# A convolution stage in which one more of eight shifted copies of its input is made on chip instead of being loaded, with the order of the copies changed

## The chip, the cores and the metric

The kernel runs on one core of one Trainium2 chip. The time is device time in microseconds of one execution; the time shown for a kernel is the median of its runs. Besides these runs there is one execution that was taken with the hardware profiler, and everything said of engines, waits and transfers comes from it.

## The reference: a filter over the whole image, then a 3x3 layer

The input x holds 4 images of 512 x 512 positions with 16 channels, fp32. Two layers follow each other, each added to what it got:

```python
# layer 0: zero-padded to twice the size
X = jnp.fft.rfft2(x, s=(2 * l1, 2 * l2), axes=(-3, -2))          # x = _gn(x), 8 groups of 2 channels
Y = jnp.einsum('...hwi,ijhw->...hwj', X, H_full)                 # H_full = h0 + spectrum of the filter
y = jnp.fft.irfft2(Y, s=(2 * l1, 2 * l2), axes=(-3, -2))[..., :l1, :l2, :]
...
# layer 1: 3x3 cosine convolution of _gn(x)
y = conv(x, kernel / kernel_norm) / input_norm
y = 1.0 - jnp.arccos(y) * (2.0 / jnp.pi)
y = y * (jnp.tanh(kernel_norm / radius) * jnp.tanh(input_norm / radius)) + bias
```

_gn is a group normalization. The filter's spectrum is that of a filter between every input and output channel, a quotient of two polynomials in both directions. So the first layer is a two-dimensional linear convolution of 512 x 512 images by 512 x 512 filters, 16 x 16 of them. It is the first layer's product over channels that takes most of the time.

## The kernel before

The work is in stages, one after the other: the filter's spectrum along one axis (filter_phase), the input's transform along that axis (forward_phase), the stage that the change touches (conv_phase, line 650), and the last stage (last_phase) with the way back and layer 1. Tiles have 128 partitions (P). A scheduler orders the instructions of each engine from the program's text, the data's dependencies and the buffers of the pools; each engine then runs its own list in order, and waits for others by semaphores.

conv_phase works on 513 rows, one for each frequency along the first axis (the first frequency has two). For each row it convolves along the other axis: 64 pieces of the filter and 64 of the input, cut up as 8 by 8 to suit the tiles. The steps of a row n, each with its place:

- load_x (L697) and load_g (L685) fetch the row's input and filter from DRAM, on SP's queue.
- turn_x (L708) makes the row's rotated transform matrix: an ACT operation (turn, L718) and a DVE operation (L720).
- x_part (L723) transforms the input: 4 matmuls (L731) into px, two tiles of PSUM, each evicted into place 0 of the tile xe. evict (L678) gives every third eviction to DVE (L681), the others to ACT (L683).
- xe (L727) is 128 partitions by 8 places by 1,024 values. The 128 partitions of place 0 are 8 blocks of 16 channels. Taken together with xl, the same values multiplied by a fixed phase, they form a list of 256 rows, and place e must hold rows 16e to 16e + 127 of that list. So each place is the list seen 16 rows further on.
- x_late (L738) makes xl on POOL: four multiplications (L752), one over the whole tile (L753), one addition (L754). It also stores place 0 and xl to a DRAM scratch of 256 rows, xf_d, by two DMAs (L745) on POOL's queue. The pool of xl has one buffer, that of xe three, xf_d is fourfold.
- half_shift (L760) fills place 4: its lower 64 partitions from the upper half of place 0, its upper 64 from the lower half of xl. Both are copies on ACT (L763) of 64 x 1,024 values.
- load_xe (L766) fills places 1 to 3 and 5 to 7 from xf_d with two DMAs on SP's queue of 1,536 KB each; the second stands behind load_g's on the queue.
- g_part (L775) transforms the filter: 32 matmuls (L783, in four groups of 8 of two halves each) into tiles pg, three banks of PSUM, evicted into gh.
- mix (L792) is the product: 32 x 4 matmuls (L799) of gh with all eight places of xe, into pm, two banks, evicted to yf in four portions.
- over_q (L812) and over_g (L842) transform back: 16 transposes (L820) into pz; then an ACT copy zq (L827) and five DVE operations (L828 to L832) for every fourth; two POOL operations zd and z (L836, L838); 8 matmuls of two halves (L857) into py, evicted to yo, and a DMA to y_d on POOL's queue (L868). px, pz and py share three banks of PSUM.

step (L876) puts these together for five rows at once, in four quarters (k = 0 to 3): mix of row n, g_part of n + 1, over_q of n - 1, x_part and x_late of n + 2 at k = 0, half_shift of n + 2 at k = 2 and 3, turn_x of n + 3, over_g of n - 2. The scheduler may depart from this where an engine is free; in the built program ACT's order in a row (from one row's px to the next) is: xe eviction, lower half of place 4, yf, turn, gh, zq, upper half of place 4, yf, gh, zq, yo, yf, gh, zq, yf, gh, zq. POOL's is: two L752, store of place 0, two L752, L753, L754, store of xl, store of y, zd, z.

Of the kernel before, what the change touches and what calls it, by code (L numbers as in the profile page):

```python
# [46 lines left out]
P = 128  # L47
N = 512
B = 4
C = 16  # L50
# [6 lines left out]
XF = F * 2 * B  # L57
# [128 lines left out]
def load_const(nc, pool, cst, name, shape=None):  # L186
    src = cst[name]
    t = pool.tile(list(src.shape), F32, name=f"c_{name}")
    nc.sync.dma_start(out=t, in_=src)
    return t  # L190
# [10 lines left out]
def bc(ap, axis, shape):  # L201
    return ap.unsqueeze(axis).to_broadcast(shape)
# [447 lines left out]
def conv_phase(tc, cst, g_d, x_d, y_d):  # L650
    nc = tc.nc
    with ExitStack() as ctx:
# [15 lines left out]
        late = load_const(nc, cp, cst, "late").rearrange("p (v f) -> p v f", v=3)  # L668
# [4 lines left out]
        rows = [(0, 0, 0), (0, 0, 1)] + [(n // P, n % P, None) for n in range(1, N)]  # L673
        n_rows = len(rows)
        state = {}
# [9 lines left out]
        def load_g(n):  # L685
            rc, r, plane = rows[n]
            g = io.tile([P, C, 8 * C], F32, name="g")
            t, w = g.rearrange("p j x -> p (j x)"), C * 8 * C
            if plane is None:
                nc.sync.dma_start(out=t, in_=dram(g_d[rc], r, 0, [w, P], [1, w]))  # L690
            else:
                for to, at in ((0, (0, 96)[plane]), (64, (64, 32)[plane])):
                    nc.sync.dma_start(out=t[to : to + 32], in_=dram(g_d[rc], r, at * w, [w, 32], [1, w]))
                    nc.gpsimd.memset(t[to + 32 : to + 64], 0.0)
            state["g", n] = g

        def load_x(n):  # L697
            rc, r, plane = rows[n]
            x = io.tile([P, B, 8 * C], F32, name="x")
            t, w = x.rearrange("p b x -> p (b x)"), B * 8 * C  # L700
            if plane is None:
                nc.sync.dma_start(out=t, in_=dram(x_d[rc], r, 0, [w, P], [1, w]))
            else:
                nc.gpsimd.memset(t[S:], 0.0)
                nc.sync.dma_start(out=t[:S], in_=dram(x_d[rc], r, plane * S * w, [w, S], [1, w]))
            state["x", n] = x
# [16 lines left out]
        def x_part(n, b):  # L723

            if b == 0:

                state["xe", n] = xep.tile([P, 8, F, 2, 2, 2], F32, name="xe")  # L727
            if b % 2 == 0:
                state["px"] = ps_f.tile([P, 2, F, 2], F32, name="px", tag="full")
            px = state["px"]  # L730
            nc.tensor.matmul(px[:, b % 2].rearrange("p f c -> p (f c)"), state["x", n][:, b],  # L731
                             state["dfs", n], start=True, stop=True)
            if b % 2:
                evict(state["xe", n][:, 0, :, b // 2], px.rearrange("p k f c -> p f c k"))
            if b == B - 1:
                del state["x", n], state["dfs", n]

        def x_late(n):  # L738

            xe = state["xe", n][:, 0]  # L740
            fl = xe.rearrange("p f h c k -> p f (h c k)")

            def store(half, t):
                at = slice(C, P) if half == 0 else slice(0, P - C)
                nc.gpsimd.dma_start(out=xf_d[n % 4][half * P :, :][at], in_=t[at].rearrange("p f x -> p (f x)"))  # L745

            store(0, fl)
            xl = xlp.tile([P, F, 2, 2, 2], F32, name="xl")
            u = xlp.tile([P, F, 2, 2, 2], F32, name="xu")
            for c in range(2):  # L750
                for h in range(2):
                    nc.gpsimd.tensor_mul(u[:, :, h, c], xe[:, :, h, 1 - c], bc(late[:, 1 + c], 2, [P, F, 2]))  # L752
            nc.gpsimd.tensor_mul(xl.rearrange("p f h c k -> p f (h c k)"), fl, bc(late[:, 0], 2, [P, F, 8]))  # L753
            nc.gpsimd.tensor_add(xl.rearrange("p f h c k -> p (f h c k)"),  # L754
                                 xl.rearrange("p f h c k -> p (f h c k)"),
                                 u.rearrange("p f h c k -> p (f h c k)"))
            store(1, xl.rearrange("p f h c k -> p f (h c k)"))
            state["xl"] = xl

        def half_shift(n, half):  # L760

            dst, src = ((slice(0, 64), state["xe", n][64:, 0]), (slice(64, P), state["xl"][:64]))[half]
            nc.scalar.copy(state["xe", n][dst, 4].rearrange("p f h c k -> p (f h c k)"),  # L763
                           src.rearrange("p f h c k -> p (f h c k)"))

        def load_xe(n):  # L766
            src = xf_d[n % 4]
            for t in (1, 5):
                nc.sync.dma_start(
                    out=state["xe", n][:, t : t + 3].rearrange("p t f h c k -> p t (f h c k)"),  # L770
                    in_=bass.AP(tensor=src.tensor, offset=src.offset + t * C * XF,
                                ap=[[XF, P], [C * XF, 3], [1, XF]]),
                )

        def g_part(n, j):  # L775


            if j % 4 == 0:
                state["pg"] = [ps_g.tile([P, 4, F], F32, name=f"pg{c}", tag="pg") for c in range(2)]
            g, pg = state["g", n], state["pg"]  # L780
            for c in range(2):
                half = slice(64 * c, 64 * c + 64)
                nc.tensor.matmul(pg[c][:, j % 4], g[half, j], dg[half], start=True, stop=True)  # L783
            if j == 3:
                state["gh", n] = ghp.tile([P, F, 2, C], F32, name="gh")
            if j % 4 == 3:
                for c in range(2):
                    evict(state["gh", n][:, :, c, j - 3 : j + 1], pg[c].rearrange("p j f -> p f j"))
            if j == C - 1:
                del state["g", n]  # L790

        def mix(n, g):  # L792

            if g % 8 == 0:
                state["pm"] = ps_m.tile([P, 8, 8, 2 * B], F32, name="pm")
            xe, gh, pm = state["xe", n], state["gh", n], state["pm"]
            for q in range(4):
                f = g + 32 * q
                nc.tensor.matmul(  # L799
                    pm[32 * q : 32 * q + 32, g % 8], gh[:, f].rearrange("p c j -> p (c j)"),  # L800
                    xe[:, :, f].rearrange("p t h c k -> p t (h c k)"), start=True, stop=True,
                )
            if g == 7:

                state["y", n] = yp.tile([P, 16, 32, 4], F32, name="yf")
            if g % 8 == 7:
                evict(state["y", n][:, :, g - 7 : g + 1].rearrange("p t g x -> p g t x"),
                      pm.rearrange("p g t (h x) -> p g (t h) x", h=2))
            if g == 31:
                del state["xe", n], state["gh", n]  # L810
# [65 lines left out]
        def step(n):  # L876


            def row(k):
                return 0 <= n + k < n_rows  # L880

            if row(3):
                load_x(n + 3)
            if row(2):
                load_g(n + 2)
            if row(1):
                load_xe(n + 1)
            for k in range(4):
                if row(0):
                    for g in range(8):  # L890
                        mix(n, 8 * k + g)
                if row(1):
                    for j in range(4):
                        g_part(n + 1, 4 * k + j)
                if row(-1):
                    for t in range(4):
                        over_q(n - 1, 4 * k + t)
                if row(2) and k == 0:
                    for m in range(B):
                        x_part(n + 2, m)  # L900
                    x_late(n + 2)
                if row(2) and k >= 2:
                    half_shift(n + 2, k - 2)
                if row(3) and k == 2:
                    turn_x(n + 3)
                if row(-2) and k == 2:
                    for m in range(4):
                        over_g(n - 2, m)

        for n in range(-3, n_rows + 2):  # L910
            step(n)
# [443 lines left out]
```

## Time and profile before

| what | value |
|---|---|
| median of 3 runs | 19,007.57 us (19,006.79 to 19,023.34) |
| profiled execution: time, span | 19,054.31 us, 19,052.5 us |
| mean granted TensorE clock | 0.957 |
| PE, DVE, ACT, POOL busy, share of the span | 91%, 60%, 51%, 61% |
| 7,400 to 12,000 us (in conv_phase): PE, DVE, ACT, POOL busy | 4,116, 2,503, 2,423, 2,927 us of 4,600 |
| same stretch: busy share of the DMA engines, GB/s | 0.87, 321 |
| loads of xe: count, size, median from issue to landing | 1,026, 1,536 KB, 10.3 us |
| conv_phase: first and last L731 matmul | 6,953 us, 16,004 us |

The profile counts an engine as busy while it computes; issuing DMAs does not count. A group's line gives the source line, the engine, the operation, the output and the inputs by tile names, the shapes, and the count; then busy us and the mean ns of one; then how long the engine was idle just before, and what ended that. In a timeline each row has the start in us, its length in us and the instruction; a bracket holds the idle time before it. "issue" is idle time that ended with no wait that the profile shows. PEld is the loading of weights, which overlaps PE's matmuls.

### The profile page before, as it was taken

What the parts mean: (1) busy time and instruction counts of PE and PEld (TensorE: products, weight loads), DVE (VectorE), ACT (ScalarE), POOL (GpSimd) and SP (SyncE); (2) the same over time, 40 slices, a digit from 0 to 9 for tenths busy, and PEclk for the clock granted to TensorE, in tenths of its full rate; (3) what the DMA queues carried; (4) which work ended last, traced back from release to release, by engine and by line L of the source; (5) the groups of instructions that cost most, each with busy time, mean ns of one, the idle gap of its engine ahead of it and who ended that gap; (6) DMA issues with size and microseconds to landing.
All of it is one profiled execution on the core that took longest, in us unless ns stands there. A gap on an engine that the chain in (4) does not pass through costs nothing. (4 is left out here: it accounts for less than half of the span.)

```text
span 19052.5 us, 536690 instructions
## 1 busy us (share of the span) xinstructions
PE 17293.1 (91%) x227020; PEld 12605.2 (66%) x227020; DVE 11398.8 (60%) x23961; ACT 9747.4 (51%) x17871; POOL 11564.3 (61%) x12445
## 2 busy tenths in 40 slices
PE   8899999999999988898888888888888888979999
PEld 5455555555554457777777777777777776868888
DVE  8877777777763335555555555555555554347656
ACT  4455555555552235555555555555555553107777
POOL 7577777777771126666666666666666664127655
PEclk7899999999999999999999999999999999999999
DMA  3755455555557668888888888888888887796321
GB/s 100 206 153 148 137 150 150 146 139 149 149 151 223 187 211 320 323 322 324 320 322 317 322 327 317 322 324 323 320 325 323 321 320 282 268 321 210 131 72 62
DMA packets 2918658, 4543.39 MB, mean 238 GB/s; under 512 B 117442, under 2 KB 2086300, under 8 KB 2809374
## 3 DMA queue, kind: packets, MB, share of 16 engines
q1 hardware_dynamic: 2686062, 3768.91, 58.5%
q0 software_dynamic: 174896, 605.89, 8.3%
q10 hardware_dynamic: 55296, 134.24, 2.1%
q8 instruction: 1789, 29.31, 0.6%
q14 instruction: 615, 5.04, 0.1%
HBM read 3031.23 MB, written 1477.31 MB: 237 GB/s over the span
## 5 line engine op out<-in xcount | busy, mean ns | idle before, releaser
L783 PE MATMUL pg<-c_dg,g 64*128 64x128 f32 x32832 | 2842.9, 291 | 320.9 <-ACT gh L683 159.5
L799 PE MATMUL pm<-xe,gh 128*32 128x64 f32 x131328 | 2403.4, 222 | 576.2 <-issue 353.1
L799 PEld LDWEIGHTS pm<-xe,gh 128*32 128x32 f32 x131328 | 2012.8, 110 | 1180.2 <-issue 996.4
L783 PEld LDWEIGHTS pg<-c_dg,g 64*128 64x128 f32 x32832 | 2283.2, 190 | 662.7 <-issue 262.5
L372 PE MATMUL pg<-c_dinv,sp 128*128 128x256 f32 x8192 | 2278.4, 426 | 294.3 <-ACT st L377 193.8
L828 DVE TENSOR_TENSOR z<-zq,pz 128x256 f32<-128x256 f32 x2052 | 862.0, 420 | 2617.2 <-ACT zq L827 2534.6
L348 DVE RECIPROCAL dn<-dn 128x256 f32<-128x256 f32 x1024 | 1790.8, 1749 | 778.3 <-POOL dn L341 778.0
L372 PEld LDWEIGHTS pg<-c_dinv,sp 128*128 128x128 f32 x8192 | 1609.9, 207 | 946.8 <-ACT st L377 215.3
L681 DVE COPY gh<-pg 128x512 f32<-128x512 f32 x2046 | 1410.5, 689 | 1294.1 <-PE pg L783 1289.6
L417 PE MATMUL pt<-ev_in,c_todd 128*128 128x512 f32 x4096 | 1970.1, 606 | 45.6 <-DMA ev_in<-g_d 27.0
L752 POOL TENSOR_TENSOR xu<-xe,c_late 128x256 f32<-128x256 f32 x2052 | 1393.4, 705 | 856.3 <-ACT xe L683 832.3
L335 ACT COPY ab<-pab 128x512 f32<-128x512 f32 x2048 | 1104.2, 592 | 1130.1 <-POOL m L355 333.3
L683 ACT COPY yf<-pm 128x512 f32<-128x512 f32 x2046 | 1210.5, 592 | 919.0 <-PE pm L799 904.3
L377 ACT COPY st<-pg 128x256 f32<-128x256 f32 x2048 | 1072.6, 623 | 1024.0 <-PE pg L372 619.3
L763 ACT COPY xe<-xl 64x1024 f32<-64x1024 f32 x513 | 538.8, 1050 | 1877.0 <-POOL xl L754 1877.0
L350 POOL TENSOR_TENSOR x<-ab,ab 128x256 f32<-128x256 f32 x1024 | 875.8, 855 | 933.6 <-ACT ab L335 907.0
L1208 PE MATMUL pc<-l_band,xn 128*128 128x160 f32 (+3 forms) x9024 | 1374.8, 309 | 65.0 <-DVE e_o L1255 64.0
L683 ACT COPY gh<-pg 128x512 f32<-128x512 f32 x2058 | 1201.2, 584 | 402.0 <-PE pg L783 393.6
L820 PE MATMUL pz<-c_ident,yf 128*128 128x128 f32 x8208 | 1378.2, 291 | 27.2 <-issue 25.4
L1208 PEld LDWEIGHTS pc<-l_band,xn 128*128 128x128 f32 x9024 | 1218.8, 197 | 224.7 <-issue 147.2
L329 PEld LDWEIGHTS pab<-c_e,u 18*128 18x128 f32 x8192 | 723.5, 188 | 809.5 <-ACT st L377 452.5
L417 PEld LDWEIGHTS pt<-ev_in,c_todd 128*128 128x128 f32 x4096 | 806.8, 198 | 669.9 <-issue 514.6
(195 smaller groups left out, 33846.4 us busy)
## 6 DMA issues: line engine op xcount, KB each, us to landing
xe<-xf_d SPq DMA_DIRECT2D x1026, 1536.0 KB, 10.3
g<-g_d SPq DMA_DIRECT2D x511, 1024.0 KB, 9.9
g_d<-st SPq DMA_DIRECT2D x64, 4096.0 KB, 34.3
ev_in<-g_d SPq DMA_DIRECT2D x1024, 256.0 KB, 4.8
g_d<-ot SPq DMA_DIRECT2D x1024, 256.0 KB, 2.9
xf_d<-xe POOLq DMA_DIRECT2D x513, 448.0 KB, 8.3
xf_d<-xl POOLq DMA_DIRECT2D x513, 448.0 KB, 5.3
x_d<-xo SPq DMA_DIRECT2D x128, 1024.0 KB, 5.1
```

What stands on the lines that cost most here:

```text
L335: nc.scalar.copy(w["ab"][n], pp[n])
L348: nc.vector.reciprocal(w["dn"], w["dn"])
L372: nc.tensor.matmul(pg[:, k].rearrange("p a x -> p (a x)"), w["sp"][:, k, c, :], dinv[:, 2 * kp + k, c, :], start=(c == 0), stop=(c == 1),)
L377: nc.scalar.copy(st[a][:, :, i].rearrange("p (q k x) -> p k q x", q=2, k=4)[:, 2 * kp : 2 * kp + 2], pg[:, :, a].rearrange("p k (q x) -> p ...
L417: nc.tensor.matmul(pt, todd[:, c, kc, hh * P : hh * P + P], ev[:, kc, c], start=(kc == 0), stop=(kc == 1),)
L681: nc.vector.tensor_copy(dst, src)
L683: nc.scalar.copy(dst, src)
L752: nc.gpsimd.tensor_mul(u[:, :, h, c], xe[:, :, h, 1 - c], bc(late[:, 1 + c], 2, [P, F, 2]))
L783: nc.tensor.matmul(pg[c][:, j % 4], g[half, j], dg[half], start=True, stop=True)
L799: nc.tensor.matmul(pm[32 * q : 32 * q + 32, g % 8], gh[:, f].rearrange("p c j -> p (c j)"), xe[:, :, f].rearrange("p t h c k -> p t (h c k ...
L820: nc.tensor.transpose(pz[:, t % 4].rearrange("p v q x -> p (v q x)"), y[:, at].rearrange("p g x -> p (g x)"), ident)
L1208: nc.tensor.matmul(pc[:, lo:hi, :].rearrange("p w j -> p (w j)"), xns[q][:, h * P + dh : h * P + dh + P], bands[dh][:, o : o + hi - lo, :] ...
```

## The change

Place 2 of xe is no longer loaded. It is copied in four pieces of 32 partitions: partitions 0 to 31 and 32 to 63 by POOL, 64 to 95 by ACT, all three from place 0, and 96 to 127 by ACT from xl. The first DMA of load_xe then brings places 1 and 3 only (1,024 KB), the second stays as it was. In the text of step, the copies from place 0 are written at k = 2 and k = 3 of the step that makes the row, and those from xl (place 4's upper half and place 2's last piece) at k = 1 and k = 2 of the step after, so that state keeps xl by row. No pool and no number of buffers is changed.

```diff
-            state["xl"] = xl
-
-        def half_shift(n, half):
-
-            dst, src = ((slice(0, 64), state["xe", n][64:, 0]), (slice(64, P), state["xl"][:64]))[half]
-            nc.scalar.copy(state["xe", n][dst, 4].rearrange("p f h c k -> p (f h c k)"),
-                           src.rearrange("p f h c k -> p (f h c k)"))
+            state["xl", n] = xl
+
+        def shift(n, copy, e, to, late, rows):
+
+            src = state["xl", n] if late else state["xe", n][:, 0]
+            copy(state["xe", n][to : to + rows, e].rearrange("p f h c k -> p (f h c k)"),
+                 src[(to + C * e) % P :][:rows].rearrange("p f h c k -> p (f h c k)"))
 
         def load_xe(n):
             src = xf_d[n % 4]
-            for t in (1, 5):
+            for t, by, many in ((1, 2, 2), (5, 1, 3)):
                 nc.sync.dma_start(
-                    out=state["xe", n][:, t : t + 3].rearrange("p t f h c k -> p t (f h c k)"),
+                    out=state["xe", n][:, t : t + 1 + by * (many - 1) : by].rearrange("p t f h c k -> p t (f h c k)"),
                     in_=bass.AP(tensor=src.tensor, offset=src.offset + t * C * XF,
-                                ap=[[XF, P], [C * XF, 3], [1, XF]]),
+                                ap=[[XF, P], [by * C * XF, many], [1, XF]]),
                 )
...
-                if row(2) and k >= 2:
-                    half_shift(n + 2, k - 2)
+                if row(1) and k == 1:
+                    shift(n + 1, nc.scalar.copy, 4, 64, True, 64)
+                if row(1) and k == 2:
+                    shift(n + 1, nc.scalar.copy, 2, 96, True, 32)
+                    del state["xl", n + 1]
+                if row(2) and k == 2:
+                    shift(n + 2, nc.gpsimd.tensor_copy, 2, 0, False, 32)
+                    shift(n + 2, nc.gpsimd.tensor_copy, 2, 32, False, 32)
+                if row(2) and k == 3:
+                    shift(n + 2, nc.scalar.copy, 4, 0, False, 64)
+                    shift(n + 2, nc.scalar.copy, 2, 64, False, 32)
```

In the built program ACT's order in a row becomes: xe eviction, lower half of place 4, yf, third piece of place 2, gh, zq, turn, yf, upper half of place 4, last piece of place 2, gh, zq, yo, yf, gh, zq, yf, gh, zq. POOL's becomes: two L752, store of place 0, two L752, L753, first piece of place 2, L754, second piece, store of xl, store of y, zd, z.

## The prediction

> **What bounds the kernel now.** The clock and the page's strip of slices come first. The granted clock is 0.957 over the span and 0.98 from 7,400 to 12,000 us, so no throttle is at work here. The convolution stage (513 rows, first L731 matmul at 6,953 us, last at 16,004 us) is the only stage that the diff touches. In its middle (7,400 to 12,000 us) PE is busy 4,116 of 4,600 us, ACT 2,423, POOL 2,927, and the DMA engines 87%. PE looks like the bound, but it idles about a tenth; what ends that idle time decides. From the starts of the L731 matmuls, a row takes 17.68 us on average, 17.20 in the median, and no less than 16.90: a tenth of the rows lie at 16.90 or under, a quarter at 16.92 or under. A floor so sharp is a fixed chain, not a mean of accidents. So I read one row in order of time (start us, length us; in brackets the idle time before it and what ended it):
>
> ```profile
> 10007.81 1.89 PE L731 MATMUL px<-dfs_n,x 128*128 128x256 f32 x8
> ...
> 10008.87 0.59 ACT L683 COPY xe<-px 128x512 f32<-128x512 f32 x1 [0.45 <-PE px L731]
> ...
> 10009.54 1.36 POOL L752 TENSOR_TENSOR xu<-xe,c_late 128x256 f32<-128x256 f32 x2 [1.07 <-ACT xe L683]
> ...
> 10012.89 1.97 POOL L753 TENSOR_TENSOR xl<-xe,c_late 128x1024 f32<-128x1024 f32 x1
> ...
> 10014.94 2.36 POOL L754 TENSOR_TENSOR xl<-xl,xu 128x1024 f32<-128x1024 f32 x1
> ...
> 10017.33 1.06 ACT L763 COPY xe<-xl 64x1024 f32<-64x1024 f32 x1 [3.70 <-POOL xl L754]
> ...
> 10018.41 0.59 ACT L683 COPY yf<-pm 128x512 f32<-128x512 f32 x1
> 10018.89 0.59 ACT L683 COPY gh<-pg 128x512 f32<-128x512 f32 x1
> ...
> 10019.37 0.39 ACT L827 COPY zq<-pz 128x256 f32<-128x256 f32 x1
> 10019.53 0.96 PEld L783 LDWEIGHTS pg<-c_dg,g 64*128 64x128 f32 x14 [0.27 <-ACT gh L683]
> ...
> 10021.30 0.68 DVE L681 COPY gh<-pg 128x512 f32<-128x512 f32 x1
> ...
> 10022.08 1.23 PE L799 MATMUL pm<-xe,gh 128*32 128x64 f32 x64 [0.39 <-ACT zq L827]
> ...
> 10024.82 1.89 PE L731 MATMUL px<-dfs_n,x 128*128 128x256 f32 x8
> ```
>
> The reader is to see a closed loop. Counted from px at 0: ACT evicts px at 1.06, POOL begins at 1.73 and finishes xl at 9.49; ACT, in order, has stood idle 3.70 us for it and copies at 9.52; only then come the yf (10.60), gh (11.08) and zq (11.56) that PE and DVE need; DVE does its five z operations and its own gh (13.49 to 14.17); PE's pm starts at 14.27, and the next px at 17.01. The record names zq for that last wait, but zq ended at 21.72 and DVE's gh at 21.98, so it was gh. Everything from px to px touches what precedes it. That this holds for all rows is in the groups of ACT from 7,400 to 16,000 us (count; busy us, mean ns; idle before, us):
>
> ```profile
> L763 ACT COPY xe<-xl 64x1024 f32<-64x1024 f32 x486 | 510.5, 1050 | 1777.4 <-POOL xl L754 1777.4
> L763 ACT COPY xe<-xe 64x1024 f32<-64x1024 f32 x486 | 508.1, 1045 | 655.7 <-DVE xe L681 655.7
> ```
>
> That is 3.66 us of waiting in each of 486 rows. The mean lies 0.78 us over the floor. From PE's idle time by releaser I find mostly "issue" there (about 1 us a row, in lumps near 1 us in a few rows) and late xe loads (0.15 us a row).
>
> [...] The trace has no large POOL copy, but its memset of 32x2048 took 1,798 ns, 0.88 ns per element[...]. [...] the page of before shows 29.31 MB in 1,789 packets, 16.4 KB each, while "issue" idle time stands before PE's matmuls. That these are late fetches behind the 87% DMA load is plausible, not shown.
>
> **The change part by part.** The order of the built program on each engine decides more than the diff. PE's and DVE's order within a row is unchanged. On ACT and POOL I find:
>
> (a) The late copy does not run a row later. The pool of xl has one buffer, so POOL's next L753 needs it released, and the scheduler puts both late copies (64 rows into place 4, 32 rows into place 2) on ACT right behind the same row's L754, where the one stood. ACT's wait for xl remains.
>
> (b) POOL's first 32-row copy stands between L753 and L754, the second between L754 and the store of xl. Only the first is on the loop. Its cost: 193 ns (L1162, a copy of 4 elements) + 1,024 x 0.88 ns gives 1.07 us, an estimate; plus the 0.08 us handover that L753 to L754 shows: +1.15. Bounds: [...] 1.98 (L753, a multiply of the same 1,024 with two inputs). A gain is excluded, since an instruction is added to an in-order engine that has no gap there. I take 1.07.
>
> (c) ACT's late part. Before: late copy, yf, gh, at steps of 1.08 and 0.48 us. After: two late copies, gh; the second yf has moved ahead of the wait. +1.08 - 0.48 = +0.60. I price the 32-row copy like the 64-row one: L694's memset of 32 rows and L704's of 64 (528 ns for 512 elements) follow the length along a row, not the rows.
>
> (d) ACT's early part: one more 32-row copy, +1.05, and turn is put off. The first gh comes 0.6 us later (4.97 to 5.6), and with it the bank that PE's second pg group waits for. I cost it at nothing: PE then reaches its third pg group near 11.8 instead of 11.2, and gh opens that only at about 13.4. Without that cover it would cost 0.6 us.
>
> (e) SP and DMA. The xe loads fall from 2 x 1,536 to 1,024 + 1,536 KB; with g 1,024, x 256, y 256 and the stores 2 x 448 a row moves 4,992 instead of 5,504 KB, 9% less. The store of xl is issued 2 x 1.15 = 2.3 us later, so the first load, the g load and the second load behind it on SP go out as much later; the second now goes at 15.8, lands at 28.6 and is wanted at 16.9 + 14.3 = 31.2. After: 18.1, 30.9 or sooner, wanted at 18.65 + 16.0 = 34.7. No new wait; the late loads should nearly vanish. Behind the store on POOL is the y store, which waits for yo anyway, and zd and z, which end 0.36 us into the next row as now, 1.4 us before POOL is next wanted.
>
> (f) POOL's total: 9.7 us of work and 1.7 of issuing, plus 2.1; ACT's 9.3 plus 2.1. Both stay under 14 us of a row: neither becomes the bound by its sum.
>
> Sum on the loop: 1.15 + 0.60 = +1.75, a floor of 16.90 + 1.75 = 18.65. Over it: if each row of before is lifted to 18.65 where it was shorter, the mean is 18.83, so 0.18 over. Stalls ahead of the chain now have 1.75 us more cover and DMA is lighter; I take half, 0.09. A row is then 18.74, +1.06; times 512 is +543 us. The profiled execution (19,054.3 us, span 19,052.5, so 1.8 around it) would become 19,597. It is 46.7 above the median of the runs, 19,007.6, to which I add the same 543: 19,550.
>
> **The rivals.** *POOL copies as slowly as it multiplies.* Strided two-input work runs at 1.93 ns per element here, and nothing of this size shows otherwise. Then (b) is 2.06, the floor 19.56, the row 19.61 with its small spread, +1.93 x 512 = +988: 19,996.
>
> *The cost follows the rows, so the relief wins (faster).* If a copy of 32 partitions cost a fraction of one of 128, say 0.27 on POOL and, against 64, half on ACT, then (b) is 0.35 and (c) 0.55 - 0.48 = 0.07: floor 17.32. With the DMA relief taking nearly all stalls (17.40), the row is 0.28 shorter: -143, 18,864. It decides once the chain grows by less than the 0.78 us that the stalls can give back. Against it: 64x1024 on ACT takes 1,050 ns and 128x512 584 to 592, so length counts.
>
> *Part of the growth is hidden.* If yf, not gh, were what PE really awaits, moving yf ahead would give back more, and only (b) would count: floor 18.05, row 18.2, +266: 19,274. Against it: the wait before pg names gh.
>
> **How the numbers follow.** Forecast 0.76; slow POOL copies 0.13; part hidden 0.06; relief wins 0.04; anything else 0.01. The range's low end is [...] floor 18.46, row 18.48, +410, so 19,418; its high end is the slow copy's 19,996. About 0.2% (38 us) is what a measurement of this kernel can tell from no change. Faster 0.04, same 0.01, slower 0.95.
>
> **What would show it.** Right: rows at a sharp floor near 18.65; ACT's wait before the xl copy near 3 us, not gone; POOL's 32-row copies at 1.0 to 1.2 us; gh and zq about 1.75 us later after px; xe loads landing well ahead; "issue" idle time mattering less. Wrong: POOL copies near 0.3 or 2 us; ACT's wait for L754 gone; or rows shorter than 17.68 with PE busy throughout.

## The result and the profile after

| | before | after |
|---|---|---|
| median | 19,014.8 us (4 runs) | 20,116.8 us (4 runs) |
| ratio | | 1.0584, 95% interval 1.0571 to 1.0596 |
| profiled execution, span | 19,052.5 us | 20,110.7 us |
| mean granted TensorE clock | 0.957 | 0.933 |
| row of the convolution (the 21st to the 491st): mean, median, lowest tenth | 17.68, 17.20, 16.90 us | 19.81, 19.92, 18.56 us |

The kernel became 1,102 us slower, where 543 was forecast; the time lies above the range. 2.13 us more in each of 512 rows is 1,093 us: practically all of it is in the convolution.

The groups of POOL and ACT from 7,400 to 16,000 us come first (count | busy us, mean ns | idle before).

```profile
L763 POOL COPY xe<-xe 32x1024 f32<-32x1024 f32 x868 | 894.2, 1030 | 55.0
L763 ACT COPY xe<-xe 32x1024 f32<-32x1024 f32 x434 | 457.6, 1054 | 10.5
L763 ACT COPY xe<-xl 64x1024 f32<-64x1024 f32 x434 | 454.2, 1047 | 1206.1 <-POOL xl L754 1205.8
L763 ACT COPY xe<-xl 32x1024 f32<-32x1024 f32 x434 | 453.4, 1045 | 5.1
```

A POOL copy of 32 rows takes 1.03 us and an ACT copy 1.05, whether of 32 or of 64 rows. ACT still waits for L754 ahead of the late copies, 2.78 us a row. That is what the prediction had. The next two views show what it did not have. First the loads of xe, on the page:

```profile
xe<-xf_d SPq DMA_DIRECT2D x513, 1536.0 KB, 12.7
xe<-xf_d SPq DMA_DIRECT2D x513, 1024.0 KB, 5.2
```

They no longer end any wait in PE's list, which is now led by others. The list of before and then that of after (who <- waited for what: us in total, times, longest; 7,400 to 16,000 us; the first has a line left out):

```profile
PE pm L799 <- issue: 330.7, 337, 3.2
...
PE pg L783 <- ACT gh L683: 142.0, 166, 2.9
PE pm L799 <- DMA xe<-xf_d: 70.0, 49, 3.0
PE pm L799 <- ACT zq L827: 58.9, 162, 0.4
```

```profile
PE pm L799 <- ACT zq L827: 661.9, 367, 2.1
PE pm L799 <- issue: 376.4, 301, 4.3
PE pg L783 <- ACT gh L683: 200.5, 201, 4.2
```

So the late loads are gone, and the waits for evictions of PSUM have grown by more: the one put down to zq from 58.9 to 661.9 us. The second view is one row of after on PE (start us, length us):

```profile
9995.42 0.65 PE L820 MATMUL pz<-c_ident,yf 128*128 128x128 f32 x4
9996.68 0.48 PE L783 MATMUL pg<-c_dg,g 64*128 64x128 f32 x2 [0.61 <-ACT gh L683]
9999.23 1.93 PE L799 MATMUL pm<-xe,gh 128*32 128x64 f32 x64 [2.06 <-ACT zq L827]
10001.10 2.07 PE L783 MATMUL pg<-c_dg,g 64*128 64x128 f32 x14
10003.10 1.11 PE L820 MATMUL pz<-c_ident,yf 128*128 128x128 f32 x4
10004.01 2.00 PE L731 MATMUL px<-dfs_n,x 128*128 128x256 f32 x8
```

and the same matmuls one row later:

```profile
10020.01 1.10 PE L799 MATMUL pm<-xe,gh 128*32 128x64 f32 x64 [0.84 <-ACT zq L827]
10021.04 1.16 PE L783 MATMUL pg<-c_dg,g 64*128 64x128 f32 x14
10022.13 0.66 PE L820 MATMUL pz<-c_ident,yf 128*128 128x128 f32 x4
10022.62 1.89 PE L731 MATMUL px<-dfs_n,x 128*128 128x256 f32 x8
```

The profile names zq for the wait of 2.06 us. But ACT's last zq ended at 9,998.66 and DVE's gh at 9,999.13, after five z operations; PE started at 9,999.23. So here too it was gh, as the prediction found in before:

```profile
9998.23 0.43 ACT L827 COPY zq<-pz 128x256 f32<-128x256 f32 x1
...
9998.45 0.68 DVE L681 COPY gh<-pg 128x512 f32<-128x512 f32 x1
```

After that wait the same 64 pm matmuls take 1.93 instead of 1.10 us, the 14 of pg 2.07 instead of 1.16. The engines by stretch (the column before the last two is the granted clock) say why:

```profile
9999.60:10004.00 4.40, 4.40 (x78) 4.00 (x70) 1.65 (x5) 1.17 (x2) 2.55 (x2) 0.50 0.92 358
10020.00:10022.60 2.60, 2.59 (x82) 2.39 (x83) 1.88 (x6) 0.95 (x2) 2.13 (x2) 1.00 0.87 302
```

PE ran at half clock: 0.50 was granted in the first stretch, 1.00 in the second. In the traces of before and after every record of the clock is of 1.0 or of 0.5, and in their convolution the half clock comes in runs of 3.41, 6.83 or 10.24 us (in before 85, 11 and 1, in after 271, 79 and 2): 3.41 us or a multiple of it. I laid PE's busy time on that grid and asked how often the next stretch ran at half clock:

```
PE busy in a stretch of 3.41 us   0.3-0.4      0.4-0.5      0.5-0.6      0.6-0.7      over 0.7
before: next one at half clock    22 of 22     49 of 56     14 of 69     0 of 197     under 1%
after:  next one at half clock    148 of 148   122 of 143   88 of 245    10 of 246    under 1%
```

In these two kernels a stretch in which PE is busy for less than about half is mostly followed by one at half clock. In after, half clock followed all 148 stretches with PE busy for 30 to 40%, and in 127 of them no single wait of PE was longer than 2.15 us. It also matters at which clock a stretch itself ran. Of the stretches of after at full clock and over 60% busy, 4 of 2,005 were followed by half clock; of those at half clock and under 80% busy, 76 of 76. So half clock, once there, took more PE work to leave than to avoid. Counting half-clock stretches that follow each other as one run, the convolution of before has 97 runs (375 us in all), that of after 352 (1,485 us). Below, a row "with half clock" is one of the 471 rows of the table in which such a run begins.

### The profile page after: what moved, and what is told of

Same layout as the page of the kernel before. It is cut to its first block, busy times and chain, and to the rows that moved or that the text cites. A ratio compares the mean times of both kernels' runs of the same rounds, so it can differ in the third digit from the quotient of the medians.

```text
span 20110.7 us, 539737 instructions
## 1 busy us (share of the span) xinstructions
PE 17628.4 (88%) x227020; PEld 12930.8 (64%) x227020; DVE 11398.5 (57%) x23961; ACT 10783.0 (54%) x18897; POOL 12590.6 (63%) x13471
## 3 DMA queue, kind: packets, MB, share of 16 engines
q8 instruction: 1789, 29.31, 0.6%
## 5 line engine op out<-in xcount | busy, mean ns | idle before, releaser
L799 PE MATMUL pm<-xe,gh 128*32 128x64 f32 x131328 | 2492.1, 227 | 1227.1 <-ACT zq L827 782.7
L783 PE MATMUL pg<-c_dg,g 64*128 64x128 f32 x32832 | 2933.4, 306 | 388.7 <-ACT gh L683 254.5
L799 PEld LDWEIGHTS pm<-xe,gh 128*32 128x32 f32 x131328 | 2098.7, 114 | 1807.3 <-issue 921.7
L783 PEld LDWEIGHTS pg<-c_dg,g 64*128 64x128 f32 x32832 | 2396.7, 204 | 721.0 <-ACT gh L683 325.3
L752 POOL TENSOR_TENSOR xu<-xe,c_late 128x256 f32<-128x256 f32 x2052 | 1388.4, 703 | 1173.9 <-ACT xe L683 1157.2
L763 ACT COPY xe<-xl 64x1024 f32<-64x1024 f32 (+1 forms) x1026 | 1072.8, 1046 | 1445.9 <-POOL xl L754 1439.5
L820 PE MATMUL pz<-c_ident,yf 128*128 128x128 f32 x8208 | 1469.1, 305 | 28.2 <-issue 26.3
L763 ACT COPY xe<-xe 64x1024 f32<-64x1024 f32 (+1 forms) x1026 | 1076.9, 1050 | 681.6 <-DVE xe L681 669.1
```

Of the source, the lines that this page charges most:

```text
L763: copy(state["xe", n][to : to + rows, e].rearrange("p f h c k -> p (f h c k)"), src[(to + C * e) % P :][:rows].rearrange("p f h c k -> p ( ...
L799: nc.tensor.matmul(pm[32 * q : 32 * q + 32, g % 8], gh[:, f].rearrange("p c j -> p (c j)"), xe[:, :, f].rearrange("p t h c k -> p t (h c k ...
L820: nc.tensor.transpose(pz[:, t % 4].rearrange("p v q x -> p (v q x)"), y[:, at].rearrange("p g x -> p (g x)"), ident)
```

## The experiments

**Theory.** Two things add up. The chain px, xe, POOL, late copies on ACT, gh and zq, DVE, pm, px closes on itself and was made longer, as predicted (+1.66 us in the shortest rows). And while PE waits for that chain, it often falls under half busy and gets half clock in the very matmuls that follow, which are on the chain too. **Rival:** the chain is all that the change does to PE, the rest has another cause (POOL, transfers, instruction fetches), and the low clock only goes with it.

**a_fill**: the changed kernel with PE kept busy in its wait. The inner edit is shown; that the first g_part of the next row runs before the pm that waits is arranged by ordering alone:

```diff
             for c in range(2):
...
-                nc.tensor.matmul(pg[c][:, j % 4], g[half, j], dg[half], start=True, stop=True)
+                for _ in range(7 if j == 0 and c == 0 else 1):
+                    last = nc.tensor.matmul(pg[c][:, j % 4], g[half, j], dg[half], start=True, stop=True)
```

> The changed kernel with PE kept busy while it waits: the first matmul of the filter's transform for the next row is issued seven times instead of once, in the place where PE waits for gh (same values written again[...]). Theory of the clock (PE, under half busy in a stretch of 3.4 us, gets half clock in the next): the floor of a row stays at 18.55, the 352 half-clock stretches of the changed kernel fall under 100, the mean row goes from 19.81 to 18.8-19.0, the time to 19,600-19,750. Rival (the long rows have another cause and the low clock only goes with it): no gain, 20,100, or up to 650 us more for the added matmuls.

Measured: 19,950.8 us (ratio to before 1.0493, 1.0477 to 1.0508); runs of half-clock stretches from 352 to 170, mean row from 19.81 to 19.40, shortest rows 18.68. More PE work (busy for 4,135 instead of 3,829 of the 4,600 us from 7,400 to 12,000 us), 166 us less time, where the theory expected some 370 to 520, and 170 runs are left where it expected under 100. Most of these, 119, begin 14 to 17 us after px, and 98 of the 119 follow a stretch in which PE counts as 60 to 90% busy, repeats included. So the rule of half busy does not hold as it stands once the work is repeats: they did not keep the clock up as their busy time says. Why is open. The rival is weakened, not settled.

**a_pool**: the changed kernel with POOL's copies behind the store of xl (the line that keeps that store as state["stored"] is left out).

```diff
+                    with tc.issue_after(state["stored"].ins):
-                    shift(n + 2, nc.gpsimd.tensor_copy, 2, 0, False, 32)
-                    shift(n + 2, nc.gpsimd.tensor_copy, 2, 32, False, 32)
+                        shift(n + 2, nc.gpsimd.tensor_copy, 2, 0, False, 32)
+                        shift(n + 2, nc.gpsimd.tensor_copy, 2, 32, False, 32)
```

> The changed kernel with POOL's two 32-row copies behind the store of xl, instead of one between L753 and L754 and one ahead of the store. Theory (the first copy lies on the loop with 1.1 us): the shortest rows go from 18.56 to about 17.95 (POOL's copy out, but the scheduler now puts yf behind the first late copy, which takes 0.48 back), PE waits less and the half clock is rarer: mean row 18.4-18.8, time 19,400-19,600. Rival (what counts is ACT's two late copies alone, or the clock): shortest rows stay at 18.5, time within 100 us of 20,117.

Measured: 19,875.6 us (1.0456, 1.044 to 1.0472). The shortest rows fall to 18.05, as the chain has it, but the time falls by 241 us only, less than expected. PE still waits for evictions in the same place, in 414 of 471 rows (in after 395) and for 1.6 us on the mean of all rows (1.5). There are fewer half-clock runs, 312, but they are longer: 1,628 us in all against 1,485. Rows without half clock take 18.23, those with it 20.10.

**a_poolfill**: a_pool and the fill of a_fill, nine instead of seven. It separates clock from chain, since most of a_pool's waiting for evictions is in one place.

> a_pool with the first matmul of the next row's filter transform issued nine times instead of once, in the place where PE stood 1.6 us waiting in 414 of 471 rows (same values again[...]). Theory of the clock: the chain of a_pool (shortest rows 18.05) is not touched, but no 3.4 us stretch is under half busy there; half-clock stretches fall from 312 to under 120, mean row from 19.37 to 18.3-18.7, time from 19,876 to 19,350-19,550: more work, less time. Rival (the low clock comes from something else): no fall in half-clock stretches, 19,850 or more.

Measured: 19,513.9 us (1.0262, 1.0247 to 1.0278), 362 less than a_pool and in the range of the theory. The stretches of a_pool and then of a_poolfill, 7,400 to 12,000 us (PE, PEld, DVE, ACT and POOL busy, then the clock, DMA share and GB/s):

```profile
7400.00:12000.00 4600.00, 3917.68 (x85598) 3162.75 (x85597) 2297.41 (x6181) 2718.52 (x4520) 3158.83 (x3092) 0.92 0.72 267
```

```profile
7400.00:12000.00 4600.00, 4285.24 (x92584) 3501.08 (x92582) 2349.11 (x6404) 2809.30 (x4678) 3282.39 (x3203) 0.98 0.75 277
```

PE is busy 368 us more and the clock goes from 0.92 to 0.98. Half-clock runs fall to 74, the mean row from 19.37 to 18.66, though its shortest rows rise to 18.20. What was changed is PE's work in a wait (the eight repeats, and one useful matmul of g_part moved ahead of pm); the orders of ACT and POOL are those of a_pool. Rows of either kind became no shorter (18.32 without half clock, 20.83 with it), there are only fewer of the second: 64 instead of 287. With this the rival falls: the low clock does not merely go with the long rows.

**b_pool** and **b_act**: the kernel before with one half of the copies each, place 2 still loaded over them, so with no relief of the DMA.

```diff
# b_pool
+                if row(2) and k == 2:
+                    for to in (0, 32):
+                        nc.gpsimd.tensor_copy(
+                            state["xe", n + 2][to : to + 32, 2].rearrange("p f h c k -> p (f h c k)"),
+                            state["xe", n + 2][to + 32 : to + 64, 0].rearrange("p f h c k -> p (f h c k)"))
# b_act
+                if row(2) and k == 3:
+                    for to, src in ((64, state["xe", n + 2][96:, 0]), (96, state["xl"][:32])):
+                        nc.scalar.copy(
+                            state["xe", n + 2][to : to + 32, 2].rearrange("p f h c k -> p (f h c k)"),
+                            src.rearrange("p f h c k -> p (f h c k)"))
```

> The kernel before with POOL's two 32-row copies added, one between L753 and L754 (place 2 still loaded, over the same values); the scheduler moves yf ahead of the late copy. Theory (chain plus clock): floor 16.90 + 1.10 - 0.48 = 17.52, half-clock stretches 150 to 250 against 97, mean row 18.2-18.8, time 19,300-19,600. Rival (the sum of the prediction, chain alone): mean row 17.7-17.9, time 19,010-19,130.

> The kernel before with ACT's two 32-row copies into place 2 added, one early, one behind the late copy (place 2 still loaded over them, POOL as before; the order on ACT is late copy, yf, added copy, gh). Theory (chain plus clock): floor 16.90 + 1.06 = 17.96, half-clock stretches 200 to 320, mean row 18.7-19.4, time 19,550-19,900, near a_pool, which differs from it in the load of place 2 and in POOL's copies behind the store. Rival (chain alone): mean row 18.1-18.3, time 19,230-19,330.

Measured, beside 19,026.0 for before, taken with them: b_pool 19,409.0 (1.0208, 1.0192 to 1.0224), shortest rows 17.49, 220 half-clock runs; b_act 19,798.5 (1.0407, 1.0389 to 1.0424), shortest rows 18.05, 265 half-clock runs. Both lie where chain and clock together were expected. The shortest rows rise by 0.59 and 1.15, together 1.74, against 1.66 in the changed kernel. The times rise by 383 and 772, together 1,155 against the change's 1,102. So the parts nearly add up. The 53 us between the sums may be what 9% less DMA is worth in the changed kernel, but nothing separates that from how the two delays act together. By the chain alone b_pool should have cost at most some 100 us.

In b_pool PE's wait lies elsewhere: ahead of an earlier pg, for gh from ACT, 452.0 us against 142.0 in the list of before. The half clock moved with it: 187 of its 220 runs begin 12 to 15 us after px, while in after most begin 14 us or later. And PE waits for xe loads for 4.8 us in all in b_pool (7,400 to 16,000 us), though it loads as much as before: a longer row is enough to hide them.

**b_late** and **a_late**: before and after, each with what comes from xl put on ACT behind the row's last but one zq, so that ACT no longer stands before gh and zq. The lines are those added to after; in b_late half_shift's second half stands in the place of the two shifts.

```diff
-                nc.scalar.copy(lo, pz[:, :, 0])
+                state["zq"] = nc.scalar.copy(lo, pz[:, :, 0])
...
+                    with tc.issue_after(state["zq"].ins) if row(-1) else ExitStack():
+                        shift(n + 2, nc.scalar.copy, 4, 64, True, 64)
+                        shift(n + 2, nc.scalar.copy, 2, 96, True, 32)
```

> The changed kernel with both copies from xl put on ACT behind the row's last but one zq, so that ACT no longer waits for POOL's addition ahead of gh and zq that PE needs; POOL as in the changed kernel. Theory (the loop runs through that wait): the floor is gone, rows are bound by PE with its own 15.8 us and its stalls, mean row 16.3-16.9, no half clock to speak of (under 50 stretches), time 18,300-18,600. Rival (PE's stalls and POOL set the row, the wait only fills idle time): a row no shorter than 17.7, time 19,000 or more.

> The kernel before with its one copy from xl put on ACT behind the row's last but one zq, nothing else changed (place 2 still loaded). Theory (the wait closes the loop in the kernel before too): floor of 16.90 gone, mean row 16.4-17.0, time 18,350-18,700; a little behind a_late if 9% less DMA helps, a little ahead if three more copies on ACT and two on POOL hurt. Rival (DMA at 87% sets the row): 5.5 MB a row at 321 GB/s are 17.1 us, so no row under 17.1 on average and 18,700 or more.

Measured: a_late 18,904.3 (0.9947, 0.9928 to 0.9966); b_late 19,020.8 (1.0005, 0.9996 to 1.0014). The sharp floor is gone in both (lowest tenth 15.76 and 16.19 us), so the wait did close the loop. But I expected 300 to 700 us of gain; a_late has 110 and b_late none: their mean rows are 17.39 and 17.62, and 141 and 147 half-clock runs are left. PE's waits in b_late and then in a_late, 7,400 to 15,700 us:

```profile
PE pm L799 <- issue: 372.4, 363, 4.0
PE pm L799 <- DMA xe<-xf_d: 229.3, 107, 5.3
PE pg L783 <- issue: 143.0, 107, 3.3
```

```profile
PE pm L799 <- issue: 363.6, 323, 3.6
PE pm L799 <- DMA xe<-xf_d: 171.0, 119, 5.6
PE pg L783 <- issue: 133.8, 84, 4.4
```

Where the floor went, the next bound came: late xe loads, 229 us in that stretch of b_late against 70 in a slightly longer one of before, and stalls named "issue", 372 against 331, with half clock behind them. How much each adds was not separated. Rows without half clock take 16.92 in b_late, those with it 19.40, and there are 133 of these against 86 before. Here the rival expectation, transfers and PE's own stalls, was nearer for b_late than mine. a_late is 116 us ahead of b_late with four more copies a row: once no copy is on the loop, loading less seems to pay.

**a_both**: a_pool's and a_late's edits together.

> The changed kernel with both remedies: POOL's two copies behind the store of xl, ACT's two copies from xl behind the row's last but one zq. No copy then lies between px and what PE waits for, and the xe loads go out some 2 us sooner than in a_late. Theory: no floor; late xe loads (0.3 us a row in a_late) all but gone; mean row 17.0-17.3 against 17.39, time 18,650-18,850, faster than all before it. Rival (what is left are PE's stalls at its instruction fetches and the half clock behind them, which no copy's place changes): as a_late, 18,850-18,950.

Measured: 18,774.1 us (0.9873, 0.9855 to 0.9891), the fastest version, 252 us under before and in the range of the theory. ACT's wait for L754 is gone (7,400 to 16,000 us):

```profile
L763 ACT COPY xe<-xl 64x1024 f32<-64x1024 f32 x486 | 514.0, 1058 | 11.9 <-POOL xl L754 0.2
L763 ACT COPY xe<-xl 32x1024 f32<-32x1024 f32 x486 | 508.0, 1045 | 5.7
```

Its PE waits now:

```profile
PE pm L799 <- issue: 420.1, 348, 4.0
PE pg L783 <- DMA g<-g_d: 127.3, 96, 4.4
PE pg L783 <- issue: 125.8, 93, 3.3
```

No xe load is late any more; the g load, which now stands behind both on SP's queue, is, a little. Most of what is left is "issue". The mean row is 17.22, rows without half clock 16.52.

## Why the prediction was wrong, point by point

**What bounded the kernel: right for the floor.** The loop through ACT's wait for L754 was there; taking the wait away removed the floor (a_late, b_late). But b_late became no faster: late loads and stalls stood right behind the loop.

**(a), the late copy does not run a row later: right.** The wait is still there, 2.78 us a row.

**(b) and (c): right in size.** (b) was priced at 1.07 plus 0.08 us and is 1.03 plus 0.06 to 0.08; its terms, 193 ns and 1,024 x 0.88 ns, make 1.09, and what stood for it in the low end of the range was the author's estimate, which no trace had shown. The late copies' start moved from 9.54 to 10.66 us after px, +1.12. gh moved from 11.10 to 12.79, +1.69. The floor was to be 18.65; the lowest tenth of the rows is at 18.56. Rows without half clock take 18.75 on average, against the predicted mean row of 18.74; that the two agree to 0.01 is luck, since 56 of those 149 rows still hold the end of a half-clock run.

**(d), the early copy at nothing: right for the chain.** The first gh came at 5.67, as said. Whether PE's short stall there takes part in a low stretch was not tried.

**(e): right that no new wait comes.** The second load goes out at 16.4 (in before at 16.1, not 15.8), earlier than the predicted 18.1; the store of xl lands in 3.4 instead of 5.3 us. Late loads vanished from PE's waits, but in b_pool they nearly did so without any relief of the DMA.

**The step that failed** is the one called "Over it", resting on the first paragraph's "so no throttle is at work here". The 0.957 and the 0.98 of the middle were read as none; there were 97 runs of half clock in the convolution. Of the 0.78 us by which before's mean row exceeded its floor, 86 of 471 rows with half clock at 19.57 against 17.26 for the others make 0.42. I put that excess down to fetches and late loads, and let it shrink to 0.09 with more cover. It grew to 1.25: 322 of 471 rows of after have half clock and take 20.30 against 18.75, which is 1.06 us a row. In after PE idles nearly as long in the rows with half clock as in the others, 3.37 and 3.20 us, so nearly all of their difference, 1.55 us, is the clock. In before it idles 2.57 and 1.69, so of the 0.42 a part is the stall itself. Together, 1.49 us more in the rows without half clock and 0.64 more from those with it are the 2.13 measured. The cover that was to absorb stalls is idle time of PE, and stretches with much of it are those that half clock followed (in after 270 of the 291 in which PE was busy for 30 to 50%). The sign and the chain were right. The term of the spread, put at 0.09, was wrong because the clock was taken to play no part.

**The rivals.** Slow POOL copies: not so, 1.03 us. Cost by rows: not so, ACT takes 1.05 us for 32 rows as for 64. Part hidden: not so; in b_pool yf moved ahead, and the shortest rows rose by 0.59, about the 1.10 of POOL's copy less the 0.48 priced under (c). None of the three spoke of the clock, and the time went past the upper end that was made with slow copies.

## What to carry to other kernels

When a chain of evictions is lengthened, cost PE's idle time twice: once as waiting, and once as half clock if PE falls under about half busy in a stretch of 3.4 us, as it did here (270 of 291 such stretches of after, at 30 to 50% busy, had half clock behind them); a mean clock a little under 1 is not nothing (0.957 over before's span held 97 runs of half clock in the convolution), so look at which rows hold it. A copy that no one needs soon should not stand, on an engine's list, ahead of evictions that PE needs: a scheduler that sees it ready puts it there, whatever the source says, so read the built order and pin the copy behind them. Taking bytes off the DMA paid only after the copies that replace them were off the loop (a_late, a_both), and taking the wait away paid only with fewer bytes (a_late, not b_late).

## What the runs showed of the hardware that was not expected

- Useless matmuls in a wait made a kernel 362 us faster (a_pool to a_poolfill), while the mean clock of the stretch shown rose from 0.92 to 0.98.
- The long stalls ascribed to "issue" come at one place of the program. Counting PE's and PEld's records in order, semaphore records among them, all 384 of before's over 0.5 us fall on the same place in each 256 instructions, and so do all 365 of a_late; in after 410 of 589 do, so there the name covers other waits too. The page of before has a DMA queue of kind "instruction" (q8: 1,789 packets, 29.31 MB, 16.4 KB each), and PE's and PEld's records there are 458,096, some 256 to a packet. So the stalls look like waits for these packets; that each ended with one was not shown. 29% of such crossings of before, from one 256 to the next, stall for over 0.5 us, 1.26 us on average, 1.0 us a row.
- These stalls did not follow the DMA load, as I had thought plausible: 29% of crossings with the DMA engines 87% busy (before), 31% at 71% (after), 18% at 84% (b_pool), 35% at 79% (b_act). What decides which crossing stalls stays open.
- Half clock, once there, held on: in a_pool all 162 half-clock stretches with PE under 80% busy were followed by another, while none of the 2,023 at full clock and over 60% busy was followed by one.
